# A state space layer: summing over the states by matmuls with the identity in place of accumulated transposes

## The chip, the cores and the metric

One core of a Trainium2 chip runs the whole program. The metric is the device time of one execution in microseconds (us); several executions are timed and the median is quoted. PE is the matmul engine, DVE the vector engine, ACT the scalar engine, POOL the general-purpose engine.

## The reference, cut to what matters

Two layers act on a tensor of 4 x 384 x 64 x 64 floats. The first is a Mamba-like state space layer, the second a 7 x 7 neighbourhood attention, which the change does not touch. In the first layer each of 768 channels carries 16 states, over 4096 tokens per image:

```python
def step(h, inp):
    dt_t, B_t, C_t, x_t = inp
    dA = jnp.exp(dt_t[:, :, None] * A[None])
    dBx = (dt_t * x_t)[:, :, None] * B_t[:, None, :]
    h = dA * h + dBx
    y_t = jnp.einsum('bdn,bn->bd', h, C_t)      # the sum over the 16 states
    return (h, y_t)
...
y = jnp.moveaxis(ys, 0, 1) + xc * D              # the skip
y = y * _silu(z)                                  # the gate
out = jnp.einsum('bld,cd->blc', y, out_proj_w)    # the output projection
```

## The kernel before

Channels lie on partitions, tokens in the free dimension. The work goes in 64 chunks (`STEPS`) of 256 tokens (`T`). A chunk has six blocks of 128 channels (`d`), taken as three pairs (`p`), and each block has four groups of four states (`g`). So a chunk has 24 groups (`m`) and 96 scans. Its plan has 48 **slots**; a slot is half a group, two scans on DVE, and every other piece of work is put into a slot by number, counted from the chunk's first scan (slot 48 is slot 0 of the next chunk). Each engine runs its own instructions in that order.

For a group, ACT makes the decay tile `da` in PSUM, DVE or POOL the drive `db`, DVE scans into `hs`, and POOL multiplies `hs` by C in place:

```python
def scans(I, m, half, hs):
    ...
        nc.vector.tensor_tensor_scan(
            hs[:, j, :], da[:, k, :], dbs[I, m][:, j, :],
            state[:, d, n : n + 1] if I % NCHUNK else 0.0, ALU.mult, ALU.add)

def with_c(I, m, h, hs):
    nc.gpsimd.tensor_copy(state[:, d, g * NG : (g + 1) * NG], hs[:, :, T - 1])
    nc.gpsimd.tensor_tensor(hs, hs, h["C"][g], ALU.mult)
```

PE then sums over the states. It transposes each 128 x 128 block of `hs` and accumulates the transposes in PSUM, tokens on partitions. ACT copies the sum out, PE turns it back, adds the skip, and DVE gates it:

```python
def summed(I, m, h, hs):
    ...
            nc.tensor.matmul(
                y[:, d % 2, half, :], hs[:, k, half * P : (half + 1) * P], ident,
                is_transpose=True, ...)

def turn(I, p, h, at, s):            # s = 20, 36, 52 for the three pairs
    at(s, out)                       # nc.scalar.copy(ys, y)
    at(s + 1, back)                  # transposes with ident, then the skip matmuls with dsd
    at(s + 4, gated)                 # nc.vector.tensor_tensor(yg, y, sz, ALU.mult)
```

The projections of the next chunk, the convolution and the output projection of the chunk before share PE with this. Four PSUM banks (`ps`) serve them, one bank holds y, two hold decay tiles.

## Time and profile before

| | before |
|---|---|
| median of the three timed executions | 8371.19 us (8366.02 to 8371.4) |
| first layer, first to last scan (from the trace) | 5906.7 us |
| DVE's idle time between those scans, all gaps added up | 115.5 us |
| time at half the TensorE clock between those scans | 1303 us |

The trace comes from a further execution, of 8359.57 us. This is the view of waits, 1000 to 5000 us: who waited for whom, us in total, times, longest.

```profile
ACT da L96 <- DVE hs L571: 735.8, 1045, 2.1
PEld y L594 <- POOL hs L581: 709.8, 360, 4.1
PE y L594 <- POOL hs L581: 582.1, 310, 3.8
...
DVE hs L571 <- ACT da L96: 53.9, 70, 1.2
...
DVE hs L571 <- POOL hs L581: 10.0, 40, 0.3
```

The large waits are those of ACT and PE, which have time to spare. The scans on DVE, which set the pace, wait little: 54 us for decay tiles, in 4000 us.

### The profile page before, as it was taken

The numbers are of one execution on the slowest core, as the hardware profiler recorded it, in microseconds if no ns is written. First come the engines' busy times: TensorE is split into PE (matmuls) and PEld (weight loads), VectorE is DVE, ScalarE is ACT, GpSimd is POOL, SyncE is SP. The second block draws the span as 40 slices with busy tenths as digits, with TensorE's granted clock in tenths as the row PEclk, the third lists the DMA queues.
The fourth block names the chain that finished last, engine by engine and source line by source line (L and its number), as shares of the span: only waits on it lengthen the run. The fifth ranks groups of instructions, "written<-read, shape, count | busy, mean of one in ns | idle before, by whom it ended". The sixth has DMA issues, their size and how long they took to land. (4 is left out here: it accounts for less than half of the span.)

```text
span 8357.8 us, 139186 instructions
## 1 busy us (share of the span) xinstructions
PE 7252.0 (87%) x45882; PEld 5495.0 (66%) x45882; DVE 7311.7 (87%) x13300; ACT 5812.2 (70%) x13758; POOL 7092.7 (85%) x5719
## 2 busy tenths in 40 slices
PE   7888888888888888888888888888699999999999
PEld 5776677777666677776777677766555555555555
DVE  5999999999999999999999999999856666666666
ACT  5777777777777777777777777777545455455455
POOL 4999999999999999999999999999767677777677
PEclk9998898889889998899898889989799999999999
DMA  3111211121112111211211111112122232232222
GB/s 112 59 61 66 75 58 55 63 74 58 62 66 74 53 58 66 72 58 64 68 63 53 58 65 60 55 57 71 65 89 86 76 94 88 78 92 85 83 87 65
DMA packets 327504, 583.06 MB, mean 70 GB/s; under 512 B 62940, under 2 KB 211180, under 8 KB 326660
## 3 DMA queue, kind: packets, MB, share of 16 engines
q1 hardware_dynamic: 326788, 574.17, 21.3%
q8 instruction: 370, 6.06, 0.3%
q14 instruction: 346, 2.83, 0.1%
HBM read 471.49 MB, written 84.73 MB: 67 GB/s over the span
## 5 line engine op out<-in xcount | busy, mean ns | idle before, releaser
L571 DVE TENSOR_TENSOR_SCAN hs<-da,state,db 128x256 f32<-128x256 f32 x5760 | 3855.0, 728 | 88.9 <-ACT da L96 64.8
L96 ACT ACTIVATE da<-dt,nega 128x256 f32<-128x256 f32 x6144 | 2917.7, 477 | 1208.2 <-DVE hs L571 1100.8
L581 POOL TENSOR_TENSOR hs<-hs,C 128x1024 f32<-128x1024 f32 x1536 | 3621.7, 2358 | 123.9 <-POOL state L580 0.4
L594 PE MATMUL y<-ident,hs 128*128 128x128 f32 x12288 | 1774.6, 296 | 904.5 <-POOL hs L581 902.3
L594 PEld LDWEIGHTS y<-ident,hs 128*128 128x128 f32 x12288 | 1540.5, 153 | 1207.9 <-POOL hs L581 1098.9
L941 POOL TENSOR_SCALAR sg<-sg,rsum 128x308 f32<-128x308 f32 x1536 | 1619.9, 1073 | 633.8 <-DVE rsum L939 631.8
L550 POOL TENSOR_TENSOR db<-dtx,B 128x1024 f32<-128x1024 f32 x576 | 1360.5, 2362 | 0.1
L550 DVE TENSOR_TENSOR db<-dtx_ps,B 128x1024 f32<-128x1024 f32 x960 | 1141.3, 1199 | 0.0
L382 PE MATMUL mm_ps<-xn,w_in 128*128 128x256 f32 x4608 | 1127.4, 392 | 10.1 <-DVE yg L624 8.1
L96 ACT ACTIVATE sg<-sg,mx 128x308 f32<-128x308 f32 x1536 | 828.7, 541 | 251.3 <-DVE mx L926 236.7
L926 DVE CUSTOM_DVE_ANT_0 sg<-lg_ps,bias 128x308 f32<-128x308 f32 x1536 | 643.1, 475 | 375.1 <-PE lg_ps L920 375.1
L382 PEld LDWEIGHTS mm_ps<-xn,w_in 128*128 128x128 f32 x4608 | 872.5, 197 | 119.1 <-DVE yg L624 8.4
L389 PE MATMUL mm_ps<-xb,dcv 128*128 128x256 f32 x3072 | 783.9, 409 | 0.0
L389 PEld LDWEIGHTS mm_ps<-xb,dcv 128*128 128x128 f32 x3072 | 615.7, 208 | 88.3 <-issue 0.3
L969 ACT COPY tb<-pt_ps 88x512 f32<-88x512 f32 x384 | 222.2, 579 | 624.7 <-PE pt_ps L965 624.7
L580 POOL COPY state<-hs 128x4 f32<-128x4 f32 x1536 | 289.1, 188 | 341.8 <-DVE hs L571 328.0
L639 PE MATMUL mm_ps<-yg,w_out 128*128 128x256 f32 x2304 | 539.8, 385 | 0.0
L956 DVE COPY ta<-pt_ps 110x512 f32<-110x512 f32 x768 | 492.4, 682 | 23.2 <-PE pt_ps L951 23.2
L639 PEld LDWEIGHTS mm_ps<-yg,w_out 128*128 128x128 f32 x2304 | 439.6, 195 | 59.1
L951 PE MATMUL pt_ps<-ident,sg 128*110 128x128 f32 x3072 | 417.7, 279 | 0.8 <-POOL sg L941 0.8
L951 PEld LDWEIGHTS pt_ps<-ident,sg 128*110 128x110 f32 x3072 | 322.7, 133 | 77.9 <-issue 47.6
L824 PE MATMUL mm_ps<-xn,w_qkv 128*128 128x512 f32 (+2 forms) x612 | 270.7, 579 | 60.4 <-DVE xn L811 53.2
(141 smaller groups left out, 9152.5 us busy)
## 6 DMA issues: line engine op xcount, KB each, us to landing
B<-bcrows SPq DMA_DIRECT2D x256, 512.0 KB
C<-bcrows SPq DMA_DIRECT2D x256, 512.0 KB
vw<-vd SPq DMA_DIRECT2D x1792, 33.0 KB
xr<-x SPq DMA_DIRECT2D x28, 1056.0 KB
vd<-v SPq DMA_DIRECT2D x280, 96.0 KB
xi<-in_x_dram SPq DMA_DIRECT2D x64, 384.0 KB
xo<-in_x_dram SPq DMA_DIRECT2D x64, 384.0 KB
x<-xo SPq DMA_DIRECT2D x64, 384.0 KB
```

The source lines that it names most:

```text
L96: ins = nc.scalar.activation(o, i, func, **kw)
L382: nc.tensor.matmul(pb[:, k, :], w_in[:, j, m * P : (m + 1) * P], xn[:, j, :], start=(j == 0), stop=(j == NJ - 1),)
L389: nc.tensor.matmul(pb[:, k, :], dcv[:, d, c, :], xb[:, d, c : c + T], start=(c == 0), stop=(c == KC - 1),)
L550: eng.tensor_tensor(db, dtx.unsqueeze(1).broadcast_to([P, NG, T]), h["B"][g], ALU.mult)
L571: nc.vector.tensor_tensor_scan(hs[:, j, :], da[:, k, :], dbs[I, m][:, j, :], state[:, d, n : n + 1] if I % NCHUNK else 0.0, ALU.mult, ALU.add,
L581: nc.gpsimd.tensor_tensor(hs, hs, h["C"][g], ALU.mult)
L594: nc.tensor.matmul(y[:, d % 2, half, :], hs[:, k, half * P : (half + 1) * P], ident, is_transpose=True, start=(first and half == 0 and d % ...
L639: nc.tensor.matmul(h["po", first][:, m - first, :], w_out[:, d, m * P : (m + 1) * P], h["yg"][d // 2][:, d % 2, :], start=(d == 0), stop=( ...
L926: nc.vector.tensor_tensor_reduce(sg[:, hh, :], lg[:, :NK], bias[:, 4 * m + hh, :], -1.0, BIG, ALU.add, ALU.min, mx[:, hh : hh + 1],)
L941: nc.gpsimd.tensor_scalar(sg[:, hh, :], sg[:, hh, :], rs[:, hh : hh + 1], None, ALU.mult)
L951: nc.tensor.transpose(pt[: KN[c], col : col + P], sg[:, 2 * pair + hh, KOFF[c] : KOFF[c] + KN[c]], ident,)
L956: nc.vector.tensor_copy(t[: KN[0], :, :].rearrange("p a q -> p (a q)"), pt[: KN[0], :])
```

## The change

The sum is taken without transposing: the identity is the stationary operand and `hs` the moving one, so y comes out with channels on partitions and needs neither the copy nor the turning back. It is done half a group at a time, six slots behind the scans. The gate reads y where PE summed it.

```diff
-            def summed(I, m, h, hs):
+            def summed(I, m, half, h, hs):
                 d, g = divmod(m, NS // NG)
-                ...
-                        nc.tensor.matmul(
-                            y[:, d % 2, half, :], hs[:, k, half * P : (half + 1) * P], ident,
-                            is_transpose=True, ...
-                        )
-
-            def turn(I, p, h, at, s):
-                ...                      # ACT's copy, the transposes back, the skip, the gate
+                k = d % 2
+                if half == 0 and k == 0 and g == 0:
+                    h["y", d // 2] = ps_y.tile([P, 2, T], F32, tag="y", name="y")
+                y = h["y", d // 2][:, k, :]
+                if half == 0 and g == 0:
+                    nc.tensor.matmul(
+                        y, dsd[:, d, :], h["xc"][d // 2][:, k, :], start=True, stop=False
+                    )
+                for j in (2 * half, 2 * half + 1):
+                    nc.tensor.matmul(
+                        y, ident, hs[:, j, :], start=False,
+                        stop=(g == NS // NG - 1 and j == NG - 1),
+                    )
 ...
+            LAG, FIRST, GATE, HS = 6, 9, 7, 6
 ...
-                    turn(I, p, h, slot_of(I), (p + 1) * (SLOTS // 3) + 4)
+                    slot_of(I)(
+                        (p + 1) * (SLOTS // 3) + GATE, lambda I=I, p=p, h=h: gated(I, p, h)
+                    )
 ...
+            def sums(slot, n):           # called with n = 2 in every slot
+                for _ in range(n):
+                    ...
+                    at, rest = waiting[0]
+                    if slot < at + (LAG if at % PER else FIRST):
+                        return
+                    waiting.pop(0)
+                    summed(*rest)
```

The first half group of a pair is held to nine slots (`FIRST`), the gate moves from slots 24, 40, 56 to 23, 39, 55 (`GATE`), and `hs` gets six buffers instead of five.

More of the change, by code (lines that the diff above doesn't have):

```diff
@@ L581, in with_c @@
                 nc.gpsimd.tensor_tensor(hs, hs, h["C"][g], ALU.mult)
-            def summed(I, m, h, hs):
+            def summed(I, m, half, h, hs):
                 d, g = divmod(m, NS // NG)
-                if d % 2 == 0 and g == 0:
-                    h["yt"][d // 2] = ps_y.tile([P, 2, 2, P], F32, tag="y", name="y")
-                y = h["yt"][d // 2]
-                for k in range(NG):
-                    first = g == 0 and k == 0
-                    last = g == NS // NG - 1 and k == NG - 1
-                    for half in range(2):
-                        nc.tensor.matmul(
-                            y[:, d % 2, half, :], hs[:, k, half * P : (half + 1) * P], ident,
-                            is_transpose=True, start=(first and half == 0 and d % 2 == 0),
-                            stop=(last and half == 1 and d % 2 == 1), skip_group_check=True,
-                        )
@@ L600, in turn @@
-            def turn(I, p, h, at, s):
-                def out():
-                    h["ys", p] = w2.tile([P, 2, 2, P], F32, tag="ys", name=f"ys_{I}_{p}")
-                    nc.scalar.copy(h["ys", p], h["yt"][p])
-                def back():
-                    h["y", p] = bank()
-                    for k in range(2):
-                        y = h["y", p][:, k, :]
-                        for half in range(2):
-                            nc.tensor.matmul(
-                                y[:, half * P : (half + 1) * P], h["ys", p][:, k, half, :], ident,
-                                is_transpose=True, start=(k == 0 and half == 0), stop=False,
-                                skip_group_check=True,
-                            )
-                        nc.tensor.matmul(
-                            y, dsd[:, 2 * p + k, :], h["xc"][p][:, k, :], start=False,
-                            stop=(k == 1), skip_group_check=True,
-                        )
-                def gated():
-                    yg = w2.tile([P, 2, T], F32, tag="yg", name=f"yg_{I}_{p}", bufs=4)
-                    nc.vector.tensor_tensor(yg, h["y", p], h["sz"][p], ALU.mult)
-                    h["yg"].append(yg)
-                at(s, out)
-                at(s + 1, back)
-                at(s + 4, gated)
@@ L631, in out_proj, with gated @@
+            def gated(I, p, h):
+                yg = w2.tile([P, 2, T], F32, tag="yg", name=f"yg_{I}_{p}", bufs=4)
+                nc.vector.tensor_tensor(yg, h["y", p], h["sz"][p], ALU.mult)
+                h["yg"].append(yg)
             def out_proj(I, h, at):
@@ L679, in layer0 @@
             STEPS = NB * NCHUNK
-            steps = [{"yg": [], "yt": {}, "dtx": {}} for _ in range(STEPS)]
+            LAG, FIRST, GATE, HS = 6, 9, 7, 6
+            steps = [{"yg": [], "dtx": {}} for _ in range(STEPS)]
             SLOTS = 2 * ND * NS // NG
@@ L737, in layer0 @@
             decay(*halves[0], steps[0])
-            behind = []
+            PER = 2 * M // (ND // 2)
+            waiting = []
+            def sums(slot, n):
+                for _ in range(n):
+                    if not waiting:
+                        return
+                    at, rest = waiting[0]
+                    if slot < at + (LAG if at % PER else FIRST):
+                        return
+                    waiting.pop(0)
+                    summed(*rest)
             for n in range(STEPS * M):
                 I, m = divmod(n, M)
-                hs = w2.tile([P, NG, T], F32, tag="hs", name=f"hs_{I}_{m}", bufs=5)
+                hs = w2.tile([P, NG, T], F32, tag="hs", name=f"hs_{I}_{m}", bufs=HS)
                 for half in range(2):
-                    if 2 * n + half + 1 < len(halves):
-                        nxt = halves[2 * n + half + 1]
+                    slot = 2 * n + half
+                    if slot + 1 < len(halves):
+                        nxt = halves[slot + 1]
                         decay(*nxt, steps[nxt[0]])
-                    if half == 0:
-                        if behind:
-                            with_c(*behind[-1])
-                        ready = len(behind) - 1
-                        if ready == 1 and behind[0][1] % (2 * NS // NG) == 0:
-                            ready = 0
-                        for _ in range(ready):
-                            summed(*behind.pop(0))
+                    if half == 0 and n:
+                        with_c(*kept_back)
+                    sums(slot, 2)
                     scans(I, m, half, hs)
                     run(I, 2 * m + half, 2 * m + half + 1)
-                behind.append((I, m, steps[I], hs))
-            with_c(*behind[-1])
-            for what in behind:
-                summed(*what)
-            run(STEPS)
+                for half in range(2):
+                    waiting.append((2 * n + half, (I, m, half, steps[I], hs)))
+                kept_back = (I, m, steps[I], hs)
+            with_c(*kept_back)
+            for slot in range(2 * STEPS * M, 2 * STEPS * M + SLOTS):
+                sums(slot, 2)
+                run(STEPS, slot % SLOTS, slot % SLOTS + 1)
     def layer1(x1s, mvs, gms):
```

## The prediction

> **What bounds the kernel now.** I read first the page's busy shares, then the busy tenths in 40 slices: slices 0 to 28 are the first layer (the changed one), the rest is the second, which the change does not touch.
>
> ```profile
> PE 7252.0 (87%) x45882; PEld 5495.0 (66%) x45882; DVE 7311.7 (87%) x13300; ACT 5812.2 (70%) x13758; POOL 7092.7 (85%) x5719
> ...
> PE   7888888888888888888888888888699999999999
> ...
> DVE  5999999999999999999999999999856666666666
> ...
> PEclk9998898889889998899898889989799999999999
> ```
>
> In the first layer DVE is at 9 tenths throughout, PE at 8, with a granted clock below full. Next, busy time by stretch: for the steady stretch 1000 to 2000 us, and for one chunk of 256 tokens cut in three (see below).
>
> ```profile
> core 0: us, PE busy (x) PEld busy (x) DVE busy (x) ACT busy (x) POOL busy (x), PEclk, DMA share, GB/s
> ...
> 1000.00:2000.00 1000.00, 851.83 (x4456) 707.78 (x4455) 980.26 (x1437) 783.96 (x1721) 919.93 (x693) 0.89 0.19 63
> ```
> ```profile
> 2905.29:2933.19 27.90, 24.41 (x134) 21.02 (x135) 27.52 (x39) 20.36 (x46) 27.23 (x21) 0.94 0.01 3
> 2933.19:2965.22 32.03, 25.65 (x129) 20.07 (x128) 30.63 (x47) 26.60 (x54) 28.92 (x23) 0.84 0.15 49
> 2965.22:2997.79 32.57, 28.20 (x149) 23.88 (x149) 32.47 (x49) 26.28 (x62) 29.37 (x24) 0.90 0.34 118
> ```
>
> DVE is busy 980 of 1000 us: it is the bound of layer 0, by its scans. A chunk takes 92.5 us (from the starts of the scans), 64 chunks 5907 us. Adding up DVE's gaps between first and last scan gives only 115 us for the whole layer, so removing waits cannot gain 2% (167 us). The groups view shows what feeds and follows the scans:
>
> ```profile
> L571 DVE TENSOR_TENSOR_SCAN hs<-da,state,db 128x256 f32<-128x256 f32 x5760 | 3855.0, 728 | 88.9 <-ACT da L96 64.8
> L594 PE MATMUL y<-ident,hs 128*128 128x128 f32 x12288 | 1774.6, 296 | 904.5 <-POOL hs L581 902.3
> L382 PE MATMUL mm_ps<-xn,w_in 128*128 128x256 f32 x4608 | 1127.4, 392 | 10.1 <-DVE yg L624 8.1
> ```
>
> The decisive reading is in the counts. The program makes 64 x 24 x 8 = 12288 transposing matmuls in the sum: one record each. It makes 64 x 36 = 2304 calls in the input projection: **two** records each. And the timeline gives the pitch:
>
> ```profile
> 3000.48 1.46 PE L382 MATMUL mm_ps<-xn,w_in 128*128 128x256 f32 x6
> ...
> 3001.77 1.04 PE L594 MATMUL y<-ident,hs 128*128 128x128 f32 x8
> ```
>
> (1.46 - 0.38)/5 = 0.216 us per ordinary record, where 0.38 is one record's modelled length; (1.04 - 0.27)/7 = 0.110 us per transposing record. Start-to-start times over the whole layer agree: medians of 216 and 109 ns at full clock, 427 and 213 at half.
>
> **What the Trainium skill says.** "FP8 and Floating Point Precision", TensorE Precision Notes: true FP32 takes four passes through the array. The trace fits: two records of 216 ns for 256 columns, about four times 256 columns at full clock. "Perfetto Trace Analysis", Transposes: a logical transpose should use the transpose, not a standard matmul, as it has logic to skip the arithmetic. The trace fits: 128 columns in 109 ns, in one record. So the old form moves 256 tokens of a state in 0.22 us, the new one takes 0.43. "PSUM — Partial Sum Buffer", The four PSUM rules: a first matmul clears the written bits of the whole bank but not the data. So the second channel half's start does no harm to the first half, which is complete by then; no run shows this yet. "Perfetto Trace Analysis", Identifying the Most-Contended Engine: PE's busy share is no measure of its headroom; I therefore count records times pitch.
>
> **The change part by part.**
> 1. *Sum.* Removed per chunk: 24 groups x 8 x 0.109 = 20.9 us of PE. Added: 24 x 4 matmuls x 2 records x 0.216 = 41.5 us.
> 2. *Turning back.* Removed per chunk: 12 transposes, 1.3 us of PE, and 3 copies of 0.58 us on ACT. The skip matmuls (12 records) only move.
> 3. *The rest of PE* per chunk, from counts of calls: input projection 72 records, convolution 48, output 36, six smaller kinds 48 with the skip: 204 x 0.216 = 44.1 us. PE goes from 44.1 + 22.2 = 66.3 us (72%) to 85.6 us (93% of 92.5) at full clock.
> 4. *ACT's copies.* In the timeline of one chunk ACT waits for DVE both before and after the copies, except near slot 22 (a slot is two scans, 48 to a chunk), where the copy makes a decay tile late and DVE loses 0.25 us: 16 us over the layer. DVE's larger repeating gap (0.86 us at slot 39, 55 us in all) comes from softplus pieces on ACT and stays.
> 5. *Lag and buffers.* Sums come at six slots behind a scan, not about four, so PE waits less for POOL's multiplication; a sixth hs buffer pays for it. But y has one bank, read directly by the gate. A loop arises: gate of pair p-1 (after the scans of slot 7 of its third) frees the bank, PE sums 16 half groups of pair p with all its other work in between, then DVE may gate pair p (after slot 23). PE can no longer work ahead across a gate.
>
> The loop for each pair, PE work between gates against DVE time (cuts at slots 8, 24, 40, median of chunks 17 to 43: 27.4, 32.0, 33.2 us):
> - sums and skip are 64 + 4 records in each.
> - Slots 8 to 24: z projection 36 and output projection 24 between: 128 records, (127 x 0.216) + 0.42 to the landing + 0.1 for the release = **27.95 us**. DVE takes 27.4 less the 0.62 gate, which has moved by one slot: **26.8 us**. PE is late by 1.2 us.
> - Slots 24 to 40: some 26 other records: 20.3 us plus 3.9 us of leftover output projection and mean, against 31.4: slack.
> - Slots 40 to 8: 60 other records, 27.95 against 32.5: slack, but PE idles some 6 us before it. In the records of before, a half clock follows a 3.4 us stretch with under about half of PE's time used, so this loop should start at half clock and lose 0.9 to 2.5 us; then the last convolution (16 records, 3.5 us) ends about when the gate opens, or up to 0.6 us late.
>
> So DVE stalls before the second gate of each chunk by 1.2 us plus some 0.2: about 1.4 us x 63 = 88 us (the last chunk has no successor to prepare). This already includes the 0.25 us gap of slot 22, which becomes part of the wait. At the layer's end PE's chain to the last gate is about 1.3 us shorter. Sum: +87.
>
> **Rivals.**
> - *DVE stays the bound and only the copies' cost goes*: 0.25 us per chunk and the tail, 8371 - 17 = 8354. For it: 7% of PE remains free over a chunk. Against it: the first third's loop has no room by the count above; it takes an error of 4% in that count to save it.
> - *PE becomes the bound everywhere*, through half clock or late projections that hold up ACT and so the decay tiles. For it: before, PE ran at half clock for about 1307 us of layer 0; if the first third had one such 3.4 us stretch per chunk, each would cost another 1.7 us, and the time would be about 8371 + 64 x 3.1 = 8570. Against it: that third begins with hardly any idle PE time, and a fuller PE keeps its clock. The evacuations I checked have from 0 to 10 us to spare; the first-third z tile (ready 12.9 us after the gate, wanted at about 13.5) and the first convolution of the next chunk are tight.
> - *PE gains, as 256 columns per matmul halve the instruction count*: that would be so if a plain fp32 matmul were one record of 216 ns (0.86 us per group against 0.87), and the time about 8354 again. The two records per call in L382 speak against it; the skip matmuls, of the very shape and form of the new ones with a diagonal matrix, have two as well (768 records for 384 calls).
>
> **Range and chances.** The mechanism rests on counted records and measured pitches; the size of the stall is a small difference of two large numbers (28.0 and 26.8), each good to perhaps 0.4 us, with the clock adding on one side only. A stall of 0.5 to 2.8 us per chunk gives 8403 to 8550. I predict 8458, range 8400 to 8550. Faster by 2% would need 167 us, more than all idle time of DVE: 0.01. Slower by 2% needs 2.6 us per chunk: 0.14. Within 2%: 0.85.
>
> **What the profile after should show.** The sum as about 12288 records of 128x256, pitch 216 ns, two per matmul. PE busy in layer 0 rising from 85% to 93% or more, its granted clock rising above 0.89, its idle time on POOL's product shrinking from 902 us. ACT down by 111 us, 192 fewer instructions. DVE's busy time unchanged, about 980 falling to some 966 per 1000 us; a new wait of DVE's gate (yg) for PE's y, of 1 to 2 us, in one of three gates, the one after slot 23; hardly any at the other two. A chunk of 93.9 us. The second layer unchanged within 3 us. I am wrong if the new matmuls have one record, if DVE's new waits are at scans for decay tiles rather than at the gate, or if all three gates wait.

## The result, and the profile after

| | before | after |
|---|---|---|
| median, same rounds | 8368.62 us | 8409.02 us (8406.8 to 8411.53) |
| ratio, 95% interval | 1 | 1.0048 (1.0031 to 1.0066) |
| first to last scan | 5906.7 us | 5952.5 us |
| DVE idle there | 115.5 us | 160.8 us |
| half clock there | 1303 us | 287 us |

A ratio is the mean time of one kernel's fast executions over that of the other's of the same rounds, so it is not quite the ratio of the medians quoted. The last three rows are of one traced execution each. What follows the first layer's last gate takes from 2328 to 2338 us in the traces of all the runs, with both forms of the sum; so a few us of difference between two traces need not come from an edit. The change costs 0.5%: neither 2% slower nor nothing, and half of what was predicted. From the page of the kernel after: busy time, busy tenths in 40 slices, granted clock, and the groups of the sum and the skip.

```profile
PE 7992.7 (95%) x45114; PEld 6132.9 (73%) x45114; DVE 7311.7 (87%) x13300; ACT 5738.6 (68%) x13566; POOL 7089.8 (84%) x5719
...
PE   7999999999999999999999999999799999999999
...
PEclk9999999999999999999999999999899999999999
...
L596 PE MATMUL y<-hs,ident 128*128 128x256 f32 x12288 | 3064.7, 391 | 10.5 <-POOL hs L581 10.5
...
L592 PE MATMUL y<-xc,dsd 128*128 128x256 f32 x768 | 265.3, 430 | 234.1 <-DVE yg L603 234.0
```

PE gained 741 us of busy time and DVE none (7311.7 in both). The sum has as many records as before, but each of 256 columns: 6144 matmuls, two records each. The idle time of PE has moved: 10.5 us instead of 902 before the sums, where it waits for POOL, and 234 us, which is new, before the skip matmul that opens a pair, where it waits for the gate to free y. The view of waits, 1000 to 5000 us, shows the other end of that coupling:

```profile
ACT da L96 <- DVE hs L571: 788.5, 1099, 2.3
PEld y L592 <- DVE yg L603: 168.4, 52, 3.9
PE y L592 <- DVE yg L603: 148.0, 46, 3.5
...
DVE yg L603 <- PE y L596: 44.2, 43, 3.0
DVE hs L571 <- ACT da L96: 41.0, 50, 1.1
```

DVE's gate now waits for PE's sum, 43 times in some 43 chunks; before, DVE's gate waited for PE once in the whole layer, 8.3 us at its end. Two of these waits in DVE's timeline (start, duration, engine, line, names; in brackets the idle time before it and who ended it):

```profile
2293.31 1.38 DVE L571 TENSOR_TENSOR_SCAN hs<-da,state,db 128x256 f32<-128x256 f32 x2
2296.36 0.69 DVE L603 TENSOR_TENSOR yg<-y,sz 128x512 f32<-128x512 f32 x1 [1.67 <-PE y L596]
...
2387.29 1.38 DVE L571 TENSOR_TENSOR_SCAN hs<-da,state,db 128x256 f32<-128x256 f32 x2
2389.09 0.69 DVE L603 TENSOR_TENSOR yg<-y,sz 128x512 f32<-128x512 f32 x1 [0.42 <-PE y L596]
```

The second, 0.42 us, is the wait of an ordinary chunk; the first is that of a chunk in which PE began the pair 1.4 us late. Sorted by slot, the waits lie before the gate that follows slot 23 and add up to 65.4 us between the first and the last scan. DVE's gap near slot 22 (17.5 us over the layer before) is gone: it had been put down to POOL, but the scan there starts 0.60 us after the end of its decay tile in every chunk, to within 2 ns (at slot 39, where ACT ends the wait, 0.54 us), and ACT makes that tile behind this copy and the one of `dtx`, without idle time between. It went away with the copy and remains in e8 and e9, which keep it. 65.4 less 17.5 is 48 us, against 45 us by which all of DVE's idle time rose.

### The profile page after: what moved, and what is told of

It reads as the page before. It is cut to its first block, busy times and chain, and to the rows that moved or that the text cites.

```text
span 8404.7 us, 136524 instructions
## 1 busy us (share of the span) xinstructions
PE 7992.7 (95%) x45114; PEld 6132.9 (73%) x45114; DVE 7311.7 (87%) x13300; ACT 5738.6 (68%) x13566; POOL 7089.8 (84%) x5719
## 4 chain that ended last, share of the span: by engine, by line
PE 53%; DVE 22%; POOL 13%; issue 6%; ACT 5%; DMA 0%; SPq 0%; POOLq 0%; DVEq 0%; ACTq 0%
PE y L596 14%; DVE hs L571 13%; POOL hs L581 8%; PE mm_ps L382 5%; PE mm_ps L389 4%; PE pt_ps L940 4%; PE lg_ps L909 3%; PE mm_ps L813 3%; PE mm_ps L993 3%; PE mm_ps L846 3%; PE mm_ps L876 3%; DVE db L550 3%; PE pv_ps L966 3%; ACT da L96 3%; POOL db L550 3%
## 5 line engine op out<-in xcount | busy, mean ns | idle before, releaser
L596 PE MATMUL y<-hs,ident 128*128 128x256 f32 x12288 | 3064.7, 391 | 10.5 <-POOL hs L581 10.5
L596 PEld LDWEIGHTS y<-hs,ident 128*128 128x128 f32 x12288 | 2390.8, 196 | 442.7 <-issue 67.5
L550 DVE TENSOR_TENSOR db<-dtx_ps,B 128x1024 f32<-128x1024 f32 x960 | 1143.8, 1202 | 0.0
L389 PE MATMUL mm_ps<-xb,dcv 128*128 128x256 f32 x3072 | 714.7, 378 | 1.4 <-DVE gm_b L268 1.4
L389 PEld LDWEIGHTS mm_ps<-xb,dcv 128*128 128x128 f32 x3072 | 581.1, 189 | 84.4 <-DVE gm_b L268 2.2
L592 PE MATMUL y<-xc,dsd 128*128 128x256 f32 x768 | 265.3, 430 | 234.1 <-DVE yg L603 234.0
```

The costliest lines, as they stand in the source:

```text
L389: nc.tensor.matmul(pb[:, k, :], dcv[:, d, c, :], xb[:, d, c : c + T], start=(c == 0), stop=(c == KC - 1),)
L550: eng.tensor_tensor(db, dtx.unsqueeze(1).broadcast_to([P, NG, T]), h["B"][g], ALU.mult)
L596: nc.tensor.matmul(y, ident, hs[:, j, :], start=False, stop=(g == NS // NG - 1 and j == NG - 1),)
```

## The experiments

All give correct results. Ratios are to the kernel before, which ran in the same rounds. Added up from the traces, between the first and last scan: DVE's idle time, its wait before the gate after slot 23, PE's half clock; and the **late start**, from the end of the gate after slot 7 to PE's first skip matmul of the next pair (a mean without the first and last few chunks). Idle times are good to about 2 us. An empty field was not read out.

| run | median us | ratio (95%) | DVE idle | wait at that gate | half clock | late start |
|---|---|---|---|---|---|---|
| the change | 8409.02 | 1.0048 (1.0031 to 1.0066) | 160.8 | 65.4 | 287 | 0.76 |
| e1 | 8453.71 | 1.0105 (1.0092 to 1.0119) | 209.8 | 112.4 | 263 | 0.21 |
| e2 | 8582.77 | 1.0260 (1.0246 to 1.0274) | 317.6 | 163.5 | 471 | 2.54 |
| e3 | 8352.88 | 0.9984 (0.9972 to 0.9997) | 105.3 | 0.0 | 181 | 0.46 |
| e4 | 8396.60 | 1.0036 (1.0024 to 1.0049) | 142.9 | 47.2 | 44 | 0.40 |
| e5 | 8358.12 | 0.9989 (0.9976 to 1.0003) | 108.7 | 4.9 | 191 | 0.48 |
| e6 | 8397.94 | 1.0037 (1.0024 to 1.0050) | 147.4 | 85.4 | 164 | 0.20 |
| e7 | 8325.01 | 0.9950 (0.9937 to 0.9962) | 74.3 | 0.0 | 147 | 0.20 |
| e8 (old sum) | 8370.78 | 1.0003 (0.9991 to 1.0016) | 124.0 | | | |
| e9 (old sum) | 8337.74 | 0.9966 (0.9953 to 0.9980) | 81.8 | | 1202 | |
| e10 = e7 | 8326.44 | 0.9954 (0.9942 to 0.9967) | 74.6 | 0.0 | | |
| e11 = e9 (old sum) | 8335.38 | 0.9965 (0.9952 to 0.9979) | 81.5 | | | |
| e12 | 8326.92 | 0.9956 (0.9943 to 0.9968) | 67.0 | 0.0 | | 0.17 |

**What was in question.** The trace after shows the predicted wait at the predicted gate, but smaller. Measured from gate to gate in an ordinary chunk, PE takes what was predicted: 27.99 us, with 128 records, against 27.95. DVE takes 27.57 us (27.99 less its wait of 0.42) and not 26.8. The timeline of DVE in slot 7 shows why (start, duration, engine, line):

```profile
2266.46 0.66 DVE L603 TENSOR_TENSOR yg<-y,sz 128x512 f32<-128x512 f32 x1
2267.04 1.21 DVE L550 TENSOR_TENSOR db<-dtx_ps,B 128x1024 f32<-128x1024 f32 x1
2268.18 2.02 DVE L571 TENSOR_TENSOR_SCAN hs<-da,state,db 128x256 f32<-128x256 f32 x3
```

When the gate moved from slot 8 to slot 7 it came to stand *ahead* of a db multiplication in that slot, which takes 1.14 us from start to start. So DVE has this to do between the two gates, and I had left it out. The theory to test is the loop: gate, PE's sums with the work between them, gate. The rival is that PE's load over a chunk sets the time, wherever the pieces lie.

### e1: the gate behind the multiplication in slot 7

```diff
-                for p in range(ND // 2):
+                for p in range(ND // 2 - 1):
                     slot_of(I)((p + 1) * (SLOTS // 3) + GATE, ...)
 ...                                  # after everything else has been put into the slots:
+            for I in range(STEPS):
+                slot_of(I)(SLOTS + GATE, lambda I=I, h=steps[I]: gated(I, 2, h))
```

> Only edit: the gate of the third pair (slot 7) is queued behind the 1.2 us db multiplication of the same slot on DVE instead of ahead of it; no work is added. Theory (a loop from gate to gate, in which I left out this multiplication when I sized DVE's time): DVE has 1.2 us less between the gates of slots 7 and 23, so the wait before the gate after slot 23 goes from 0.42 us in an ordinary chunk to 1.6 us; the late starts (mean 0.65 us) shrink to 0.1-0.2, as PE has 1.2 us more before; mean wait 1.07 -> 1.75 us, total about 43 us more than the changed kernel, ratio to before about 1.010. Rival (PE's total load per chunk sets the time, not the loop): the same order of work and the same load, ratio stays 1.005.

Measured: ratio 1.0105, 45 us more than the change. The wait in an ordinary chunk is 1.55 us, and the late start shrinks to 0.21 us. Two neighbouring instructions of one engine changed places, no work was added, and it cost 0.6%. DVE's timeline of one chunk, gate to gate:

```profile
2289.71 1.20 DVE L550 TENSOR_TENSOR db<-dtx_ps,B 128x1024 f32<-128x1024 f32 x1
2290.83 0.68 DVE L603 TENSOR_TENSOR yg<-y,sz 128x512 f32<-128x512 f32 x1
...
2319.50 0.69 DVE L603 TENSOR_TENSOR yg<-y,sz 128x512 f32<-128x512 f32 x1 [1.55 <-PE y L596]
```

The loop is confirmed, and so is the size of the term that I had left out; the rival is refuted.

### e2: two banks for y, three for the projections

```diff
-            ps_y = es.enter_context(tc.tile_pool(name="ps_y", bufs=1, space=PSUM))
-            ps = es.enter_context(tc.tile_pool(name="ps0", bufs=4, space=PSUM))
+            ps_y = es.enter_context(tc.tile_pool(name="ps_y", bufs=2, space=PSUM))
+            ps = es.enter_context(tc.tile_pool(name="ps0", bufs=3, space=PSUM))
```

> Only edit: y gets two PSUM banks, the projections three instead of four. Loop theory: PE no longer waits for a gate before the next pair's sums, the wait at the gate after slot 23 goes from 1.07 us per chunk to about 0, and the time falls to DVE's bound: before less the 0.27 us gap of slot 22, about 8350, ratio 0.998, if three banks are enough. Rival (PE's total load): the load is unchanged, the wait moves to decay tiles or projections, ratio stays at 1.005 or rises, also if three banks are too few.

Measured: 2.6% slower than before. Three banks are too few. In the waits of 2000 to 4000 us PE now stands still before projections, for a bank that the softplus still uses, up to 12 us at a time:

```profile
PE mm_ps L382 <- DVE dt L520: 112.2, 20, 11.9
PEld mm_ps L382 <- ACT dt L96: 102.0, 18, 5.7
DVE yg L603 <- PE y L596: 65.5, 36, 3.0
```

The run says nothing for or against the loop, as it brings a larger wait of its own. The layer's pools hold 2 + 1 + 1 + 4 = 8 banks; e2 keeps that number, and no run gave y a second bank without taking one from the projections.

### e3: the output projection out of the loop

```diff
-                for n, slot in enumerate((17, 18, 19, 20, 22, 23)):
+                for n, slot in enumerate((21, 22, 23, 24, 25, 26)):
```

> Only edit: the six pieces of the output projection go from slots 17-23 to 21-26, so that the loop before the gate after slot 23 holds 104 records instead of 128 (22.8 us instead of 27.95 in PE), the rest goes where PE idles before the gates of slots 23 and 39. Loop theory: the wait at that gate is 0 in nearly all chunks, late starts included; chunk 92.3 us; about 8350, ratio 0.998. Rival (total load): no change of load, ratio 1.005.

Measured: ratio 0.9984, as expected, and the wait is 0. The loop has 104 records and takes 22.7 us in PE, with 5 us to spare. The load of a chunk is the same. This alone turns the loss of 0.5% into a gain of 0.2%.

### e4: useless work on PE

```diff
+                    def first(pb, k, d=d, times=1 + 2 * (p == 0)):
+                        for _ in range(times):
+                            in_proj(pb, k, d + k, h["xn"])
+
-                    pair(("x", p), x, lambda pb, k, d=d: in_proj(pb, k, d + k, h["xn"]))
+                    pair(("x", p), x, first)
```

> Only edit: the first pair of the input projection (slots 38 and 39, before the gate after slot 39) is computed three times over, same result: 24 more records, 5.2 us more of useless PE work per chunk, where PE idles about 6 us. Theory (the late start of the first third comes from half clock that follows this idle): PE stays at full clock, the third 40 to 8 loses its half clock (3.6 us per chunk in the changed kernel), the sums of the first third start 0.1 us after the gate instead of 0.76, the wait falls from 1.07 to 0.42 us in all chunks; 41 us less than the changed kernel, 8368, ratio 1.000. Rival (PE is simply overloaded, or the late starts come from something else): 5.2 us more work makes the time the same or up to 5 us per chunk longer, ratio 1.005 to 1.04.

Measured: 8396.60 us, 12 us less than the change, with 5 us more PE work in every chunk; ratio 1.0036 instead of the 1.000 expected. (The intervals of the two ratios overlap; in the traces the stretch from first to last scan is 18 us shorter, 5934.0 us.) In ordinary chunks all came as expected: no half clock (44 us left in the layer), start 0.06 us after the gate, wait 0.42 us. The mean late start fell only from 0.76 to 0.40 us, because the last chunks of each image, and all of the last image, start late for another reason: DVE has no statistics of a next image to take there, so the third from slot 40 to slot 8 is 0.6 us shorter on DVE (32.57 us in place of 33.16) and as long on PE. Most of them start 0.5 us late, seven 1.4 us or more. So half clock is a cause of late starts, and accounts for about half of them. Busy time by stretch:

```profile
1000.00:2000.00 1000.00, 999.87 (x4555) 840.70 (x4554) 975.45 (x1430) 770.02 (x1680) 913.49 (x687) 1.00 0.19 64
2000.00:3000.00 1000.00, 999.87 (x4541) 840.85 (x4540) 980.17 (x1425) 772.01 (x1681) 917.94 (x689) 1.00 0.19 64
```

PE (the first busy figure after the stretch's length) is busy 999.87 of 1000 us, and the kernel is faster than the change, whose PE is busy 961. A busy share does not tell whether an engine is the bound.

### e5: one slot less of lag

```diff
-            LAG, FIRST, GATE, HS = 6, 9, 7, 6
+            LAG, FIRST, GATE, HS = 5, 9, 7, 6
```

> Only edit: LAG 5 instead of 6, so the last half group is summed one slot earlier and one piece of the output projection (6 records, 1.3 us) falls behind it, out of the loop: 122 records, 26.7 us in PE against 27.6 us of DVE's. Loop theory: an ordinary chunk waits 0 instead of 0.42 us at the gate after slot 23, a late start of 1.4 us leaves 0.5; mean wait about 0.2-0.3, 50 us less than the changed kernel, 8358, ratio 0.999. Rival (the longer lag is needed, because PE would otherwise wait for POOL's products): PE waits for hs rise and the time stays at 1.005 or rises.

Measured: ratio 0.9989, as expected. One projection piece falls behind the last sum and out of the loop: 122 records, 26.6 us. The wait is 0 in an ordinary chunk and 0.4 to 0.8 us after a late start of 1.4 us or more; its mean, 0.08 us, is below the 0.2 to 0.3 expected. PE does not wait more for POOL in a way that DVE feels.

### e6: the second gate one slot earlier

```diff
-                        (p + 1) * (SLOTS // 3) + GATE, lambda ...
+                        (p + 1) * (SLOTS // 3) + GATE - (p == 1), lambda ...
```

> Only edit: the gate of the second pair runs after the scans of slot 38 instead of 39. Two effects expected: it fills 0.66 of the 0.86 us in which DVE waits for a decay tile before slot 39, and it frees y about 2 us earlier, so that the loop up to slot 7 has 1.5 us more of DVE's time and the late starts of the first third vanish (0.1 us instead of 0.76). Wait at the gate after slot 23: 0.42 us in all chunks. Total 0.65 + 0.66 us per chunk less than the changed kernel: 8326, ratio 0.995. If half clock before slot 7 is not what makes the late starts, only the 0.66 are won: 8367, ratio 1.000.

Measured: ratio 1.0037, not 0.995. Both expected effects are there: DVE's gap before slot 39 fell from 54.7 to 17.8 us, and late starts are down to 0.20 us. But the time won went to the gate after slot 23, whose wait rose from 65.4 to 85.4 us. The trace shows how: PE is now done early and idles before slot 9, so the half clock falls at the start of the first third, where there is no room. PE's timeline of one chunk has 3.19 us of idle time before the skip matmul, then eight records of the sum in 2.80 us, and further on eight in 1.89:

```profile
2456.66 0.70 PE L592 MATMUL y<-xc,dsd 128*128 128x256 f32 x2 [3.19 <-DVE yg L603]
2457.19 2.80 PE L596 MATMUL y<-hs,ident 128*128 128x256 f32 x8
...
2461.90 1.89 PE L596 MATMUL y<-hs,ident 128*128 128x256 f32 x8
```

In chunks with full clock the gate waits 0.42 us, in those with 3.4 us of half clock in that third it waits 2.11 us. A half clock of that length loses half of it, 1.7 us: 0.42 + 1.7 = 2.1. I had moved the idle time and not thought of the clock that follows it.

### e7: e3 and e6 together

> e3 and e6 together. No wait at a gate, and the gap before slot 39 filled: e3's 0.9984 less 0.66 us x 64 = 42 us: about 8310, ratio 0.993. If the two gains are the same one, ratio 0.998.

Measured: ratio 0.995, a smaller gain than the 0.993 expected, by some 13 us. 0.28 us of the gap before slot 39 stays where 0.20 was expected, which is 5 us. The rest is DVE's own busy time between first and last scan: 5798.8 us against 5790.8 in e3. With the gate moved it rises by as much in e6 (5800.8 against 5792.9 in the change); why, no run shows. With the output projection out of the first loop, 3.4 us of half clock there do no harm: PE takes 24.4 us, DVE 27.5. In eight chunks it is 5.7 us, and DVE then waits 0.4 us for a decay tile near slot 21.

### e8 and e9: the same slot in the kernel before

Does e7's second gain need the change? In the kernel before, e8 moves only the second gate from slot 40 to 38:

```diff
-                at(s + 4, gated)
+                at(s + 4 - 2 * (p == 1), gated)
```

> The kernel before with only the gate of the second pair moved from slot 40 to 38. It tells how much of e7's gain has nothing to do with the change: the 0.86 us gap before slot 39 is filled by 0.66, 42 us: 8325, ratio 0.995, if the gap in the kernel before is the same one; no gain if the gate there has to wait for PE's turning back.

Measured: 1.0003. The gate there waits for PE's turning back, 60.5 us in all, and the gap stays in another name. e9 moves the copy and the turning back one slot earlier as well:

```diff
+                e = p == 1
-                at(s, out)
-                at(s + 1, back)
-                at(s + 4, gated)
+                at(s - e, out)
+                at(s + 1 - e, back)
+                at(s + 4 - 2 * e, gated)
```

> e8 with the second pair's copy on ACT and PE's turning back one slot earlier as well (35 and 36), so that the gate at slot 38 finds its input ready. If the wait of 0.95 us at e8's gate came only from the place of the copy and the turning back, the gap before slot 39 is now filled as in e7 and the kernel before gains 42 us: ratio 0.995, and e7's second gain has nothing to do with the change. If the last sum of the pair itself is not ready by then (in the kernel before it ends at slot 35.5 in the median), ACT waits for PE, decay tiles come late, and the ratio stays at 1.000 or rises.

Measured: 0.9966, against the 0.995 expected. The wait at the gate is gone, and as in e7 DVE's busy time took back some of the gain (5800 us between the scans against 5793). So most of e7's gain over the kernel before is to be had with the old sum.

### e10, e11, e12: the two forms side by side, and one gap more

e10 is e7 and e11 is e9, on one chip. e12 is e7 with one more edit:

```diff
-                (26, 1), (26, 1), (30, 0), (33, 1), (36, 0), (39, 1), (40, 0), (43, 1),
+                (26, 1), (26, 1), (30, 0), (33, 1), (36, 0), (38, 1), (40, 0), (43, 1),
```

> e7 again, beside e9 on one chip, to tell whether the rebalanced new form beats the old form with the same gap filled. From DVE's idle time between the first and last scan (74 against 82 us) and the shorter end of the layer the new form should be about 10 us ahead: ratio 0.995 against 0.997 for e9. If the two differ by less than their intervals, the new sum is worth nothing that these runs can show.

> e9 again on the chip of e10, so that the two can be compared round by round: ratio 0.997, some 10 us behind e10; equal to e10 if the new form of the sum is worth nothing.

> e7 with the db multiplication of slot 39 moved to slot 38 as well, to fill the remaining 0.28 us gap of DVE before slot 39: up to 18 us, ratio 0.993. If the decay tile of slot 40 is then late instead, the gap only moves and the ratio stays at 0.995.

Measured: e10 8326.44 us (8323.46 to 8328.96), e11 8335.38 us (8333.41 to 8336.47). The two do not overlap: the new sum, rebalanced, is 9 us ahead of the old one, 0.1%, with 74.6 against 81.5 us of idle time on DVE. The old form keeps its gap near slot 22 (17.5 us); the new one has more at slot 26 (16 us against 4) and less at slot 28 (11 against 17). This compares one tuned version of each form: whether the old one's 17.5 us near slot 22 could be had as well was not tried, and that is more than the 9 us. e12 gained nothing (8326.92 us): the gap before slot 39 is filled, and DVE's idle time fell by only 7 us, as other gaps grew by some 11 us, 9 of them before slots 41 and 42. So the gap moved in part, as the expectation allowed; DVE's busy time rose by the 7 us that were left (5804.5 against 5797.4 in e10).

## Why the prediction was right or wrong

The prediction named the mechanism and was wrong in size: +87 us forecast, +40 us measured.

**Right.** An ordinary fp32 matmul has two records of 216 ns and a transposing one a single record of 109 ns; the sum has 12288 records of 256 columns; PE fills up (85% to 96% busy in layer 0), its clock rises (0.89 to 0.98), it hardly waits for POOL any more. A loop from gate to gate arises through the one bank of y. Only one of the three gates waits in an ordinary chunk, the one after slot 23, and PE's side of that loop is 27.99 us against 27.95 predicted. The gap near slot 22 vanished. The rival of one record per matmul fell with the record counts, that of a PE-bound layer with e1 and e3.

**The step that failed** is "DVE takes 27.4 less the 0.62 gate, which has moved by one slot: **26.8 us**. PE is late by 1.2 us." Moving the gate by one slot moved it ahead of a db multiplication. The right sum is 27.39 - 0.60 for the gate + 1.14 for the multiplication - 0.33 for slot 22, which lasts so much less without the copy: 27.6 us, and 27.57 was measured. So an ordinary chunk waits 0.42 us; less the old gap of 0.27 near slot 22 it loses 0.15 us, and not the 1.2 forecast. e1 put the multiplication back where I had had it, and the wait became 1.55 us. The order of instructions on DVE could have been compared line by line between the two kernels before predicting; I looked at the cut positions by slot number alone.

**A second term was mis-sized the other way.** "Some 0.2" us per chunk for late starts measured 0.65 (0.76 less the 0.1 of an immediate release). The half clock does follow the idle before slot 39's gate, as predicted, but in about one chunk of four it lasts 6 us, and then the next third starts about 1.4 us late; I had taken at most 0.6. And I overlooked that the last chunks of an image have less DVE work in the third before. Together: 0.42 + 0.65 less the old gap of 0.27 is 0.8 us per chunk, against 1.4 in the prediction and 45.3/63 = 0.72 by DVE's idle time. The two errors have opposite signs: had the first stood alone, the forecast would have missed by more.

**Smaller misses.** DVE's busy time was to fall to 966 per 1000 us and fell to 970 to 978, as the stalls are half as long. ACT's busy time fell by 74 us, not 111: its records overlap, so that a copy's length is not what it takes away. PE's chain from the last scan to the last gate is 1.3 us shorter, as predicted (7.7 us against 9.0). What follows it took 4.7 us more in the one trace of each kernel, instead of under 3; it differs by up to 10 us between traces of the same form of the sum, so this is not shown to come from the change.

**On the pages cited.** "PSUM — Partial Sum Buffer", The four PSUM rules, says that a first matmul clears the bits of the whole bank and leaves the data: the second block's skip matmul opens its half of the bank with a start after the first block's sums are complete, and all runs gave correct results. "Perfetto Trace Analysis", Transposes, advises the transpose for logical transposes: here the transposes were a way to sum at half the PE time per element, and giving them up cost PE 19 us per chunk, an estimate from records times pitch at full clock. That an fp32 matmul takes four passes, which the prediction cites and finds to fit, no run shows: the trace has two records for it, and twice a transpose's time per column.

**What stays open.** Whether a second bank for y would do as well as e3 was not tried without taking a bank from the projections (e2). The six `hs` buffers and the nine slots of `FIRST` came with the change and were not varied. How the half clock picks its moment is seen only in the records: I did not vary it other than by e4 and e6.

## What to carry to other kernels

Where two engines hand a single buffer back and forth, size the loop on both sides, instruction by instruction and in the order in which each engine will run them: on which side of the hand-over a piece stands counts, though no work is added (e1: 45 us), and so does moving pieces out of the tight part of the loop (e3: 56 us gained, with the same load). Look for the stretch of the period with the least slack, not at the busy share over the whole. Idle time of an engine off the bound is not free of effect: where it is moved, it can bring the clock's fall with it to a place where it hurts (e4, e6).

## What the Trainium skill lacked or had wrong

- "TensorE: Matmul & The Clock Gate", Part 4: PE-mode transpose, says, beside figures for bf16, that full clock does not engage for transposes, as they do not count as PE-busy in the same way. The clock's records last whole multiples of 3.41 us. Cut along them, between first and last scan of the kernel before, 24 stretches at full clock had other matmuls in under 35% of their time and, with the transposes, over 60% (records times pitch); none was followed by half clock, while all 168 stretches with under 35% in all were. So fp32 transposes counted.
- No page read for this gives the share of busy time below which the clock falls. Cut in the same way, half clock followed all 168 stretches at full clock with under 35% in the kernel before, 46 of 164 with 35 to 60%, and none of 1015 above; in the kernel after 62 of 62, 2 of 14 and none of 1581. So no single share divides them, and the prediction's "under about half" holds for 203 of 246 stretches.
- "FP8 and Floating Point Precision", TensorE Precision Notes, gives four passes for true FP32 but no time and no form in the trace: two records of 216 ns for 256 columns at full clock, 427 ns at half, against one record of 109 ns for an fp32 transpose of 128 columns.
- "Perfetto Trace Analysis", Identifying the Most-Contended Engine, takes the occupancy of the vector engine, and for PE the share of peak arithmetic and the weight-load share, as guides. In e4 the weight-load share is 84% and PE's matmul share 100%, in the change 80% and 96%, and e4 is faster; that section does not speak of the slack within a period, which decided here.
